# Two-layer image kernel: the odd groups' products with C go to buffers of their own, one pair of groups later

## Chip, core and metric

The kernel runs on one core of one Trainium2 chip. The metric is the device time of one execution in microseconds (us). Before the change three runs gave 21083.03, 21088.51 and 21097.53 us, so the median is 21088.51 us. All arithmetic is in 32-bit floats.

## The reference, cut to what matters

There are 16 images of 64x64 positions with 96 channels, and two layers, each added to its input after a group normalisation. Layer 0 resamples the image, passes it through a matrix, a quadratic and a second matrix, and resamples it back. Layer 1 is a selective scan in four directions; its core is all that the change touches:

```python
delta = softplus(dts + dt_bias)                    # per channel and position
def step(h, (dt, u, b, c)):                        # one position after another
    h = exp(dt * A) * h + (dt * u) * b             # 192 channels x 16 states, 4 directions
    y = sum_n(h * c)                               # read out with C
    return h, y
...
y = y0 + y2 reversed + (y1 + y3 reversed, turned)  # 4 directions of 4096 positions
out = layernorm(y) * silu(z) @ out_proj
```

So there are three large elementwise works per state and position: the drive (dt * u) * b, the recurrence over positions, and the product of h with c, which is then summed over the states.

## The kernel before, in words

**Tiles.** A tile of the scan has 128 partitions and T = 1024 positions: 32 channels times 4 of the 16 states. The work is cut into units (list `units`): one image has 8 steps (4 stretches of 1024 positions forwards, then 4 backwards), a step has 6 blocks, a block 4 units j = 0 to 3, one for each quarter of the states. A unit holds a pair of groups, e = 1 ("odd") and e = 0 ("even"), 32 channels each. That makes 192 units for an image and 3072 in all.

**What a unit n does.** The order of emission in the unit's loop is the order on every engine; nothing rearranges it.

- `decay` (L785): ScalarE writes exp(delta * A) for one group into a PSUM tile `da0` or `da1`; there is one of each.
- `drive` (L791): GpSimd writes (dt * u) * b for both groups into one tile `b` of 128x2048, two units ahead. Four such tiles rotate (`sc_4`).
- `recur` (L797): VectorE runs the recurrence, a scan instruction at L803 (forwards) or L805 (backwards), first for the odd group, in place into `b`, then for the even group, in place into `da0`.
- Product with C: the even group's is VectorE's (L972). The odd group's is GpSimd's (L963), in place in `b`, save in each fifth unit or so (`odd_here`; `SHARE` = 5), where it is VectorE's (L954); there the odd scan writes into `da1`.
- `keep` (L807): the last column of h is copied into `new`, the starting state of the next step. For the even group, and for the odd one when `odd_here`, ScalarE copies; otherwise VectorE does. The last step of a direction keeps nothing.
- `read_out(n - 1)` (L813): TensorE sums the products of the unit before over the states, with 16 matmuls (L827) into the PSUM tile `y`.

Other work is fed into these queues in small slices at three places of each unit (`slot`): the next image's layer 0, normalisations and convolution (`front`), the last stage of the image before (`finish`), and the projections of the next step (`project`). `slot` also picks extra units for `odd_here` around the convolution (`full_unit`). Loads and stores all go through SyncE's queue, in order: `fetch_dtu`, `fetch_delta`, `fetch_bc` (tiles `bt` and `ct`, five each). A load into a tile still in use waits in that queue, and all later loads and stores with it.

On GpSimd unit n is thus: product of n (L963), drive of n+2 (L794). On VectorE: odd scan, copy, even scan, even product, with the slices' small instructions between them; among these `norm` has one 96x1 product `nb` (L237), twice for an image.

Of the kernel before, what the change touches and what calls it, by code (L numbers as in the profile page):

```python
# [45 lines left out]
F32 = mybir.dt.float32  # L46
# [16 lines left out]
T = 1024  # L63
NT = L // T
NQ = 4
QT = T // NQ
# [14 lines left out]
def tile_two_blocks(  # L81
# [4 lines left out]
    nc = tc.nc  # L86
# [21 lines left out]
    fold_s = load(fold, "fold_s")  # L108
# [509 lines left out]
    blocks = [(0, 0, 0), (0, 2, 0), (2, 0, 0), (2, 2, 1), (1, 0, 1), (1, 2, 1)]  # L618
# [4 lines left out]
    def scan():  # L623


        with ExitStack() as es:
# [1 line left out]
            up_ = es.enter_context(tc.tile_pool(name="sc_u", bufs=4))  # L628
            cp = es.enter_context(tc.tile_pool(name="sc_bc", bufs=5))
            p3 = es.enter_context(tc.tile_pool(name="sc_3", bufs=3))  # L630
            p4 = es.enter_context(tc.tile_pool(name="sc_4", bufs=4))
            p2 = es.enter_context(tc.tile_pool(name="sc_2", bufs=2))
            yp = es.enter_context(tc.tile_pool(name="sc_y", bufs=1))
            stp = es.enter_context(tc.tile_pool(name="sc_st", bufs=2))
# [96 lines left out]
            def fetch_bc(ctx, r, j, what):  # L731
                t = cp.tile([128, T], F32, name="bt" if what == 0 else "ct")
                first = NS * what + NQ * j
                nc.sync.dma_start(
                    out=t, in_=ctx["rows"][r, first:first + NQ, :].unsqueeze(0).to_broadcast([32, NQ, T])
                )
                return t
# [8 lines left out]
            units = [(si_, bi, j) for si_ in range(len(steps)) for bi in range(len(blocks)) for j in range(NQ)]  # L746
            per_step = len(blocks) * NQ
            per_image = len(once) * per_step
            ctxs = [{} for _ in steps]

            bc, dtus, deltas = {}, {}, {}
# [28 lines left out]
                v, s0, r = blocks[bi]  # L780
                return 2 * steps[st][1] + r, s0 + e if v < 2 else 4 + e

            das, bs = {}, {}

            def decay(n, e):  # L785
                k, g = group(n, e)
                da = aps.tile([128, T], F32, name="da", tag=f"da{e}")
                nc.scalar.activation(da, deltas[n // NQ, e], AF.Exp, scale=a_s[:, k, g, units[n][2]:units[n][2] + 1])  # L788
                das[n, e] = da

            def drive(n):  # L791
                b = p4.tile([128, 2, T], F32, name="b")
                bt = bc[0, blocks[units[n][1]][2], units[n][2]]
                nc.gpsimd.tensor_mul(b, dtus[n // NQ], bt.unsqueeze(1).to_broadcast([128, 2, T]))  # L794
                bs[n] = b
# [8 lines left out]
                else:  # L804
                    nc.vector.tensor_tensor_scan(out[:, ::-1], da[:, ::-1], b[:, ::-1], before, ALU.mult, ALU.add)  # L805

            def keep(n, e, h, copy):  # L807
                st, bi, j = units[n]
                if st % NT < NT - 1:
                    end = h[:, T - 1:T] if steps[st][1] == 0 else h[:, 0:1]  # L810
                    copy(states[bi][1][:, e, j:j + 1], end)  # L811

            def read_out(n):  # L813
                st, bi, j = units[n]
                _, pair, lc = steps[st]
                if j == 0:
                    ys[n // NQ] = yps.tile([128, 2, QT], F32, name="y")
                y = ys[n // NQ]
                if j == 0 and pair == 1:
                    nc.tensor.matmul(  # L820
                        y.rearrange("p e t -> p (e t)"), lhsT=ident_s, rhs=y0s.pop((lc, bi)), start=True,
                        stop=False, skip_group_check=True,
                    )
                b = bs.pop(n)
                for e in range(2):
                    for q in range(NQ):
                        nc.tensor.matmul(  # L827
                            y[32 * q:32 * q + 32, e, :], lhsT=fold_s, rhs=b[:, e, QT * q:QT * q + QT],
                            start=(pair == 0 and j == 0 and e == 0), stop=(j == NQ - 1), skip_group_check=True,
                        )  # L830

# [50 lines left out]
            def slot(position):  # L882
                nonlocal full, full_unit
                back = ahead_gen if ahead_gen.gen is not None else behind_gen
                back.at += 1
                step_gen.at += 1
                gate = back.said == WAIT and back.due() and position == 2 and storing is None
                if gate:
                    full, full_unit = 2, n + 1
                if step_gen.due() and not (full and step_gen.said == BUSY):  # L890
                    light = step_gen.said != BUSY
                    step_gen.step()

                    if light and step_gen.due() and step_gen.said != BUSY:
                        step_gen.step()
                if back.due() and (gate or back.said != WAIT):
                    back.step()
                full = max(full - 1, 0)

            last = len(units) - 1  # L900
# [10 lines left out]
                drive(n)  # L911
            for e in range(2):
                decay(0, e)
            storing, credit = None, 0

            for n, (st, bi, j) in enumerate(units):
                mi, pair, lc = steps[st]
                v, s0, r = blocks[bi]
                m = n // NQ
                if n % per_image == 0:  # L920
                    image[mi]["y"] = dram.tile([2, DI, L], F32, name="y_d")
                    behind_gen.drain()
                    ahead_gen = behind_gen = nothing
                    if mi + 1 < B:
                        ahead_gen = Background(front(mi + 1), SLICES, POS)
                elif n % per_image == 2 and mi > 0:
                    behind_gen = Background(finish(mi - 1), SLICES, POS)
                if j == 0:
                    new = stp.tile([128, 2, NQ], F32, name="new", tag=f"st{bi}")
                    states[bi] = (states[bi][1] if states[bi] else None, new)  # L930

                if j == 0:
                    ahead = None
                    if bi + 1 < len(blocks):
                        ahead = ctxs[st], bi + 1
                    elif n + NQ <= last:
                        step_gen.drain()
                        ahead = ctxs[st + 1], 0
                        next_step(st + 2, mi)
                    if ahead:  # L940
                        dtus[m + 1] = fetch_dtu(*ahead)
                elif j == 1:
                    if ahead:
                        deltas[m + 1, 1] = fetch_delta(*ahead, 1)


                credit += 1
                odd_here = n == full_unit or credit >= SHARE
                if odd_here:
                    credit -= SHARE  # L950
                h = das[n, 1] if odd_here else bs[n][:, 1, :]
                recur(n, 1, h)
                if odd_here:
                    nc.vector.tensor_mul(bs[n][:, 1, :], h, bc[1, r, j])  # L954
                keep(n, 1, h, nc.scalar.copy if odd_here else nc.vector.tensor_copy)
                if n < last:
                    decay(n + 1, 1)
                slot(0)
                if storing is not None:
                    next(storing, 0)  # L960
                    storing = None
                if not odd_here:
                    nc.gpsimd.tensor_mul(h, h, bc[1, r, j])  # L963
                if n + 2 <= last:
                    drive(n + 2)

                h = das[n, 0]
                recur(n, 0, h)
                if n >= 1:
                    read_out(n - 1)  # L970
                slot(1)
                nc.vector.tensor_mul(bs[n][:, 0, :], h, bc[1, r, j])  # L972
                keep(n, 0, h, nc.scalar.copy)
                if n < last:
                    decay(n + 1, 0)
                if n >= 1 and units[n - 1][2] == NQ - 1:
                    storing = store(n - 1)
                    next(storing)
                slot(2)
                if j == 2 and ahead:  # L980
                    deltas[m + 1, 0] = fetch_delta(*ahead, 0)
                if j == NQ - 1 and n < last and steps[units[n + 1][0]][1] == 1:
                    st2, bi2, _ = units[n + 1]
                    y0s[steps[st2][2], bi2] = fetch_y0(steps[st2][2], bi2)


                at = n % per_step
                for what in range(2):
                    ahead_j = at - (2 * NQ - 1 + what)
                    if 0 <= ahead_j < NQ:  # L990
                        bc[what, 1, ahead_j] = fetch_bc(ctxs[st], 1, ahead_j, what)
                    ahead_j = at - (5 * NQ - 1 + what)
                    if 0 <= ahead_j < NQ and st + 1 < len(steps):
                        bc[what, 0, ahead_j] = fetch_bc(ctxs[st + 1], 0, ahead_j, what)
            read_out(last)
            for _ in store(last):
                pass
# [110 lines left out]
```

## Time and profile before

| | us |
|---|---|
| Median of three runs | 21088.51 |
| Profiled execution, span from the first to the last instruction | 21083.6 |
| First and last scan instruction start, in the span | 494.0 and 20914.9 |
| GpSimd busy, VectorE busy, TensorE busy, ScalarE busy | 19498.8, 19569.4, 16908.7, 13780.9 |
| Drives, 3072 of them, mean | 4.532 |
| GpSimd's products, 2458 of them, mean | 2.358 |
| VectorE's even products, 3072, mean | 1.223 |
| Columns copied by VectorE, 1844, mean | 0.154 |
| Mean granted TensorE clock | 0.860 of full |

A group's row gives its busy time and the mean of one instruction, and after the bar the idle time of the engine just before it, with what ended that idle time. Instructions of an engine overlap a little at their ends, so the time that one costs in a full queue is the distance between the starts of its neighbours, which the timeline shows, not its own length. 3072 units lie in some 20425 us, which makes 6.649 us for one.

### The profile page before, as it was taken

The page shows a single profiled execution, that of the slowest core. Times are in us where ns is not written, and L with a number is a line of the kernel's source. Part 1 is how long each engine was busy: PE and PEld are TensorE (multiplying, and loading weights), DVE is VectorE, ACT ScalarE, POOL GpSimd, SP SyncE. Part 2 cuts the span into 40 slices and gives each one's busy share as a digit, 9 for nine tenths or more (in the row PEclk, how much of TensorE's full clock was granted, in tenths as well). Part 3 has the DMA queues.
Part 4 walks back from the last instruction along what each step waited for, and adds up shares of the span by engine and source line. Part 5 has one row for each costly group of instructions (what it writes and reads, how often), then busy time and mean ns, then how long its engine had stood idle before and what let it go on. Part 6 is the DMA issues. An engine that isn't in the chain of part 4 may idle for free. (4 is left out here: it accounts for less than half of the span.)

```text
span 21083.6 us, 273452 instructions
## 1 busy us (share of the span) xinstructions
PE 16908.7 (80%) x98988; PEld 7230.6 (34%) x98988; DVE 19569.4 (93%) x12983; ACT 13780.9 (65%) x20546; POOL 19498.8 (92%) x5538
## 2 busy tenths in 40 slices
PE   7876788888878788788788888888787787888856
PEld 4423324233343333324333242333433333243221
DVE  0999999999999999999999999999999999999997
ACT  4666666667666666666666666676666666666553
POOL 0999999999999999999999999999999999999996
PEclk8887888888889888898888988888898888988977
DMA  2565565655656566565665656556565665656654
GB/s 84 191 202 195 195 227 195 221 202 196 226 198 227 197 210 212 194 230 191 218 207 197 226 199 219 202 197 222 197 226 198 212 212 198 229 195 216 224 186 141
DMA packets 1855464, 4277.11 MB, mean 203 GB/s; under 512 B 449438, under 2 KB 548670, under 8 KB 1852062
## 3 DMA queue, kind: packets, MB, share of 16 engines
q1 hardware_dynamic: 1854110, 4259.62, 60.1%
q8 instruction: 781, 12.80, 0.3%
q14 instruction: 573, 4.69, 0.1%
HBM read 3380.58 MB, written 878.18 MB: 202 GB/s over the span
## 5 line engine op out<-in xcount | busy, mean ns | idle before, releaser
L794 POOL TENSOR_TENSOR b<-dtu,bt 128x2048 f32<-128x2048 f32 x3072 | 13895.8, 4532 | 581.2 <-DMA dtu<-dtu_d 465.1
L788 ACT ACTIVATE da<-delta,a_s 128x1024 f32<-128x1024 f32 x6144 | 6857.4, 1117 | 2562.1 <-DVE b L972 945.5
L963 POOL TENSOR_TENSOR b<-b,ct 128x1024 f32<-128x1024 f32 x2458 | 5797.1, 2358 | 836.9 <-DVE new L811 628.6
L827 PE MATMUL y<-b,fold_s 128*32 128x256 f32 x49152 | 3871.3, 437 | 1153.0 <-DVE b L972 680.8
L972 DVE TENSOR_TENSOR b<-da,ct 128x1024 f32<-128x1024 f32 x3072 | 3756.4, 1223 | 91.8
L803 DVE TENSOR_TENSOR_SCAN da<-da,new,b 128x1024 f32<-128x1024 f32 x1383 | 3245.3, 2347 | 72.7 <-ACT da L788 57.2
L805 DVE TENSOR_TENSOR_SCAN da<-da,new,b 128x1024 f32<-128x1024 f32 x1361 | 3193.0, 2346 | 99.7 <-ACT da L788 77.0
L827 PEld LDWEIGHTS y<-b,fold_s 128*32 128x32 f32 x49152 | 1388.5, 119 | 3876.9 <-issue 1464.0
L805 DVE TENSOR_TENSOR_SCAN b<-da,new,b 128x1024 f32<-128x1024 f32 x943 | 2208.7, 2342 | 139.3 <-ACT da L788 81.5
L803 DVE TENSOR_TENSOR_SCAN b<-da,new,b 128x1024 f32<-128x1024 f32 x921 | 2156.5, 2341 | 11.2 <-ACT da L788 10.5
L811 ACT COPY new<-da 128x1 f32<-128x1 f32 x2764 | 432.9, 157 | 2607.4 <-DVE b L972 2236.0
L488 PE MATMUL c_ps<-xgp,wtap_s 96*64 96x512 f32 (+1 forms) x4608 | 1728.2, 633 | 184.7 <-ACT row L506 179.4
L697 PE MATMUL s<-w,ident_s 128*128 128x512 f32 x1530 | 1167.2, 854 | 636.0 <-ACT w L692 614.2
L371 PE MATMUL h_ps<-xu,w1t_s 96*128 96x500 f32 x1920 | 1044.0, 643 | 299.9 <-ACT t L311 125.9
L383 PE MATMUL o_ps<-w2c_s,hsq 128*100 128x96 f32 x9600 | 1041.5, 266 | 178.1 <-ACT hsq L352 177.8
L677 PE MATMUL s<-pr,dtw_s 128*128 128x512 f32 x1530 | 928.5, 691 | 315.2 <-ACT delta L703 224.9
L805 DVE TENSOR_TENSOR_SCAN da<-da,b 128x1024 f32<-128x1024 f32 x482 | 1103.5, 2289 | 53.0 <-ACT da L788 43.1
L383 PEld LDWEIGHTS o_ps<-w2c_s,hsq 128*100 128x100 f32 x9600 | 975.0, 179 | 410.3 <-ACT hsq L352 232.1
L803 DVE TENSOR_TENSOR_SCAN da<-da,b 128x1024 f32<-128x1024 f32 x460 | 1053.0, 2289 | 36.8 <-ACT da L788 34.8
L697 PE MATMUL s<-e,ident_s 128*128 128x512 f32 x1530 | 1004.2, 745 | 0.0
L820 PE MATMUL y<-y,ident_s 128*128 128x512 f32 x768 | 524.2, 770 | 583.5 <-ACT yt L838 457.6
L488 PEld LDWEIGHTS c_ps<-xgp,wtap_s 96*64 96x64 f32 (+1 forms) x4608 | 583.1, 169 | 1121.7 <-issue 842.6
(143 smaller groups left out, 21936.5 us busy)
## 6 DMA issues: line engine op xcount, KB each, us to landing
dtu<-dtu_d SPq DMA_DIRECT2D x1536, 512.0 KB
delta<-delta_d SPq DMA_DIRECT2D x1536, 512.0 KB
bt<-rows SPq DMA_DIRECT2D x1024, 512.0 KB
ct<-rows SPq DMA_DIRECT2D x1024, 512.0 KB
u<-xs_d SPq DMA_DIRECT2D x893, 256.0 KB
dtu_d<-dtu SPq DMA_DIRECT2D x765, 256.0 KB
delta_d<-delta SPq DMA_DIRECT2D x765, 256.0 KB
xr<-in_x SPq DMA_DIRECT2D x768, 128.0 KB
```

The lines of the kernel that those rows point to most:

```text
L371: nc.tensor.matmul(h_ps[j], lhsT=w1t_s[:, 128 * j:128 * (j + 1)], rhs=xu.rearrange("c p q -> c (p q)"), start=True, stop=True,)
L383: nc.tensor.matmul(o_ps[:, p, :], lhsT=hsq[j][:, UPS * p:UPS * (p + 1)], rhs=w2c_s[:, j, :], start=(j == 0), stop=(j == HB - 1),)
L488: nc.tensor.matmul(c_ps[p:p + n], lhsT=wtap_s[:, tap, 128 * i:128 * i + n], rhs=xgp[:, h0:h0 + 8, dx:dx + HW], start=(tap == 0), stop=(tap ...
L677: nc.tensor.matmul(s, lhsT=dtw_s[:, pair, v, :], rhs=pr, start=True, stop=True)
L697: nc.tensor.matmul(s, lhsT=ident_s, rhs=of, start=(k == 0), stop=(k == 3))
L788: nc.scalar.activation(da, deltas[n // NQ, e], AF.Exp, scale=a_s[:, k, g, units[n][2]:units[n][2] + 1])
L794: nc.gpsimd.tensor_mul(b, dtus[n // NQ], bt.unsqueeze(1).to_broadcast([128, 2, T]))
L803: nc.vector.tensor_tensor_scan(out, da, b, before, ALU.mult, ALU.add)
L805: nc.vector.tensor_tensor_scan(out[:, ::-1], da[:, ::-1], b[:, ::-1], before, ALU.mult, ALU.add)
L827: nc.tensor.matmul(y[32 * q:32 * q + 32, e, :], lhsT=fold_s, rhs=b[:, e, QT * q:QT * q + QT], start=(pair == 0 and j == 0 and e == 0), sto ...
L963: nc.gpsimd.tensor_mul(h, h, bc[1, r, j])
L972: nc.vector.tensor_mul(bs[n][:, 0, :], h, bc[1, r, j])
```

## The change

1. The odd group's product by GpSimd is no longer in place. `weigh` writes it into a tile `p` of its own (pool `sc_p`, two tiles of 128x1024). It is issued one unit later, and behind the drive: unit n on GpSimd is now drive of n+2, product of n-1.
2. The read-out follows one unit later: `read_out(n - 2)` takes the even half from `b` and the odd half from `p` (or from `b`, where VectorE made it). With it go the store of a block's result, the start of `finish`, and the loads of the second half's `ct` tiles, which come one unit later; the loads of the next step's `ct` tiles stay where they were.
3. `sc_4` has five drive tiles instead of four.
4. ScalarE copies all last columns. For an odd group that GpSimd multiplies, the copy comes behind the decay of unit n+1.
5. The space set aside for dynamically made DMA descriptors is 1024 bytes.

```diff
-            p4 = es.enter_context(tc.tile_pool(name="sc_4", bufs=4))
+            p4 = es.enter_context(tc.tile_pool(name="sc_4", bufs=5))
+            pp2 = es.enter_context(tc.tile_pool(name="sc_p", bufs=2))
...
-            def keep(n, e, h, copy):
+            def keep(n, e, h):
                 st, bi, j = units[n]
                 if st % NT < NT - 1:
                     end = h[:, T - 1:T] if steps[st][1] == 0 else h[:, 0:1]
-                    copy(states[bi][1][:, e, j:j + 1], end)
+                    nc.scalar.copy(states[bi][1][:, e, j:j + 1], end)
+
+            def weigh(n):
+
+                _, bi, j = units[n]
+                if n not in on_vector:
+                    prods[n] = pp2.tile([128, T], F32, name="p")
+                    nc.gpsimd.tensor_mul(prods[n], bs[n][:, 1, :], bc[1, blocks[bi][2], j])
...
                 b = bs.pop(n)
+                parts_of = b[:, 0, :], prods.pop(n, b[:, 1, :])
...
-                            y[32 * q:32 * q + 32, e, :], lhsT=fold_s, rhs=b[:, e, QT * q:QT * q + QT],
+                            y[32 * q:32 * q + 32, e, :], lhsT=fold_s, rhs=parts_of[e][:, QT * q:QT * q + QT],
...
-                elif n % per_image == 2 and mi > 0:
+                elif n % per_image == 3 and mi > 0:
...
                 if odd_here:
                     credit -= SHARE
+                    on_vector.add(n)
...
-                keep(n, 1, h, nc.scalar.copy if odd_here else nc.vector.tensor_copy)
+                    keep(n, 1, h)
                 if n < last:
                     decay(n + 1, 1)
+                if not odd_here:
+                    keep(n, 1, h)
...
-                if not odd_here:
-                    nc.gpsimd.tensor_mul(h, h, bc[1, r, j])
                 if n + 2 <= last:
                     drive(n + 2)
+                if n >= 1:
+                    weigh(n - 1)
...
-                if n >= 1:
-                    read_out(n - 1)
+                if n >= 2:
+                    read_out(n - 2)
                 slot(1)
                 nc.vector.tensor_mul(bs[n][:, 0, :], h, bc[1, r, j])
-                keep(n, 0, h, nc.scalar.copy)
+                keep(n, 0, h)
...
-                if n >= 1 and units[n - 1][2] == NQ - 1:
-                    storing = store(n - 1)
+                if n >= 2 and units[n - 2][2] == NQ - 1:
+                    storing = store(n - 2)
...
-                    ahead_j = at - (2 * NQ - 1 + what)
+                    ahead_j = at - (2 * NQ - 1 + 2 * what)
...
+            weigh(last)
+            read_out(last - 1)
             read_out(last)
...
-    nc = bacc.Bacc("TRN2", target_bir_lowering=False, num_devices=1)
+    nc = bacc.Bacc("TRN2", target_bir_lowering=False, num_devices=1, dynamic_dma_scratch_size=1024)
```

More of the change, by code (lines that the diff above doesn't have):

```diff
@@ L781, in group @@
                 return 2 * steps[st][1] + r, s0 + e if v < 2 else 4 + e
-            das, bs = {}, {}
+            das, bs, prods = {}, {}, {}
             def decay(n, e):
@@ L913, in scan @@
                 decay(0, e)
-            storing, credit = None, 0
+            storing, credit, on_vector = None, 0, set()
             for n, (st, bi, j) in enumerate(units):
```

## The prediction

> **What bounds the kernel now.** I read the busy times of the engines first, then the groups, the waits of VectorE and GpSimd, and the timeline for the distances between starts.
>
> ```profile
> span 21083.6 us, 273452 instructions
> PE 16908.7 (80%) x98988; PEld 7230.6 (34%) x98988; DVE 19569.4 (93%) x12983; ACT 13780.9 (65%) x20546; POOL 19498.8 (92%) x5538
> ```
>
> Two engines are over nine tenths busy, GpSimd (POOL) and VectorE (DVE). No single one is full, so the question is what each waits for.
>
> ```profile
> POOL b L963 <- DVE new L811: 628.6, 296, 14.1
> POOL b L794 <- DMA dtu<-dtu_d: 465.1, 1, 465.1
> ...
> DVE dtu L702 <- PE s L697: 335.8, 108, 141.3
> DVE da L805 <- ACT da L788: 120.1, 115, 4.2
> DVE b L805 <- ACT da L788: 98.7, 69, 3.7
> DVE da L803 <- ACT da L788: 92.0, 85, 2.1
> DVE b L805 <- POOL b L794: 51.9, 92, 0.9
> DVE da L805 <- POOL b L794: 30.2, 42, 0.9
> ```
>
> Columns: total us, times, longest. GpSimd waits for the odd scan and its copied column (628.6). VectorE waits for GpSimd's drives only 101 us in all (51.9, 30.2 and two rows of 14.2 and 4.9). It waits for ScalarE's decays 334 us (the three rows and one of 23.6) and for TensorE's s 194 (335.8 less the one wait of 141.3 before the scan part). So inside the scan part VectorE is more often the late one, and most of its own waits are for engines that the change hardly relieves.
>
> ```profile
> 8002.47 4.54 POOL L794 TENSOR_TENSOR b<-dtu,bt 128x2048 f32<-128x2048 f32 x1
> 8002.64 0.15 DVE L811 COPY new<-b 128x1 f32<-128x1 f32 x1
> 8002.71 2.35 DVE L805 TENSOR_TENSOR_SCAN da<-da,new,b 128x1024 f32<-128x1024 f32 x1
> ...
> 8082.72 2.34 DVE L805 TENSOR_TENSOR_SCAN b<-da,new,b 128x1024 f32<-128x1024 f32 x1
> 8084.98 2.33 DVE L805 TENSOR_TENSOR_SCAN da<-da,new,b 128x1024 f32<-128x1024 f32 x1
> ```
>
> Columns: start, length. The first three lines show a copy between two scans and under a running drive. The last two show the scans of a last step, with no copy: 2.26 us from start to start.
>
> **What each engine needs.** GpSimd's product and drive repeat each 6.82 us where it never rests, and a drive alone takes 4.49. 2458 x 6.82 + 614 x 4.49 = 19520 us, of the 20425 of the scan part. The change leaves every one of these instructions; a product out of place should cost like half a drive (4.532 / 2 = 2.27 against 2.36 in place), so between -0.09 and 0 each; I take 0.
>
> VectorE needs 20425 less its waits, some 680 in the scan part (101 + 334 + 194 and about 50 in the last stage's products), so 19745. It is the busier of the two by 225 us, and gets shorter by the copies.
>
> **The change part by part.**
>
> *Copies leave VectorE.* From the odd scan's start to the even scan's start it takes 2.356 (mean, scan to copy) + 0.071 (middle value, copy to scan) = 2.427 us with a copy (1844 cases), and 2.257 without one (middle value of 510). 1844 x 0.170 = 313 us. The built program puts a wait in front of the even scan, for the product of the pair before. In 135 scan pairs of the trace such a waiting instruction stands between, and they lie 2.257 apart too: nothing.
>
> Here a rule speaks for a far greater gain. The Trainium skill, page "SBUF — State Buffer", section on SBUF's two sides, says that VectorE and GpSimd share one port pair under an exclusive lock, that a 32-bit copy within SBUF on VectorE asks for it, and that the loser stands still for the whole instruction. By that a copy under a drive waits for half of it or so, 2 us, and 1844 of them would be worth over 3000 us. The row of all 1844 copies says 153/154/157 ns (least, middle, most), under running drives too. I take the row: 313.
>
> *How much of the 313 arrives.* I cut the 14 middle images by the starts of their odd scans. In units 110 to 143 of an image (the convolution) VectorE waits 16.8 us an image for ScalarE and TensorE; 23 of an image's 115 copies lie there, and I count half of those as lost to the same waits, 23 x 16 x 0.17 / 2 = 31. Leaves 282.
>
> *Copies arrive on ScalarE.* 1844 x 0.157 = 290 us, on an engine that is 65% busy, behind the decay of n+1, which waits for the same scan. Queued behind it are the slice's work, the even copy and the even decay, for which VectorE's next even scan waits. VectorE found a decay late 295 times in 3072 units, one in ten: 29 us. If ScalarE had no slack anywhere it would be 290, if it always had, 0.
>
> *The product one unit later, behind the drive, in `p`.* Before, GpSimd can't begin product n until odd scan n is done, and the drive of n+2 stands behind it. After, a product has a unit more on both sides, and so has the drive. The products' wait of 628.6 mostly goes, but that alone gives nothing where VectorE is the late one. What it gives is VectorE's 101 us on drives. They arise where GpSimd runs without a rest: in units 144 to 169 an image takes 177.3 us with 175.6 of GpSimd's work, while just before, in 110 to 143, GpSimd idles 30.4. One unit of lead carried over covers most of these waits; I take 60 (0 to 101).
>
> *The read-out one unit later.* TensorE's 49152 matmuls stay. Before, it waits 772 us (weight loads) for L972's products just made; these waits shrink. Behind them in its queue are the slices' matmuls, which feed ScalarE and so the decays. That may shorten VectorE's 334 + 194; I count 0, and up to half, 265, as a rival. *The fifth drive tile*: the drive of n+2 takes the tile of n-3, whose read-out now stands in the same unit n-1 as that of n-2 did, so its cover is the same; the row is 87.6 us of GpSimd waiting for y. *The scratch space*: all loads are issued by SyncE, no row of GpSimd makes any; nothing.
>
> *What the lead does to `nb`.*
>
> ```profile
> L237 DVE TENSOR_TENSOR nb<-nmean,rg x32: 156/5728/12324, 38.7 to 19074.5; 96x1 f32<-96x1 f32 x32
> ```
>
> A 96x1 product takes 5.7 us in the middle and 12.3 at most, against 0.156 in the first image, where GpSimd is idle. The same page's lock covers VectorE instructions with two SBUF inputs, as this one has. By the rule it waits for one GpSimd instruction, 4.5 us at most, and a greater lead changes nothing. The timeline says more: at 7560.16 it lasts 8.14, through the rest of one drive, a product and a whole drive, and ends when GpSimd has run out of work that it may do. Thus it grows with the lead that GpSimd still has to use up. If GpSimd is mostly ahead already, by nothing; if it is just in time, by a unit and more, some 9 us, 30 x 9 = 270. VectorE being the busier, I take 1 us each, 30.
>
> *SyncE.* The next step's `ct` loads stay put while the product that frees their tile comes a unit later; see the third rival. I count 0.
>
> **Sum.** 282 + 60 - 29 - 30 = 283 less. Against the profiled 21083.6: 20801; the median of the runs is 5 above it, so 20806.
>
> **The rivals.**
>
> *More is freed* (12%): TensorE no longer waits for fresh products, and half of VectorE's 529 us on decays and s goes too. 20806 - 265 = 20541. For it: the 772 us. Against: in the convolution those waits end at ScalarE's table loads and TensorE's long matmuls, not at read-outs.
>
> *Nothing arrives* (15%): the copies' time comes back as waits for decays (up to 290), or `nb` grows by its 270. 20806 + 270 = 21076. For it: ScalarE's 334 us already there. Against: it idles a third of the time.
>
> *SyncE stalls, slower* (13%). Place: the ends of units 21, 22 and 23 of each step, where a `ct` load waits for GpSimd's product of the unit before; that wait is there now, 128 times, 75.2 us in all. Behind it stands the load of the even `delta`, due about a unit later. If GpSimd runs just in time for VectorE, the product comes up to 13.6 us later against the drives than before (drive and product twice). Then the even decay is late and VectorE with it. At 4 us a step, 128 x 4 = 512, the time is 21318. It decides from 283 / 128 = 2.2 us a step. Against: GpSimd ahead, SyncE has no wait at all; ScalarE waits for delta now only 123.9 us.
>
> **How the numbers follow.** The sum's case has 57%, with its own range 20650 to 20980 (copies' half lost or not, 0 to 101, `nb` 0 to 4 us). The rivals have 12, 15 and 13, and 3 are left for what I don't see, slower. Ten in a hundred are cut above by leaving part of the slow case out, and the low end reaches into the first rival: 20590 to 21140. A measurement tells 0.2%, 42 us, from no change. Faster: 56 of the sum's, 12, and 3 of "nothing arrives", 71%. Same: 11. Slower: 13 + 3 + 2 = 18.
>
> **What would show it.** No VectorE copy at the keep line, and odd and even scans 2.26 apart. GpSimd's wait at the products under 200 us, VectorE's at drives under 60. A mean unit of 6.56. `nb` in the middle below 8 us. VectorE's waits for decays between 300 and 400. It is wrong if SyncE's wait for GpSimd at the `ct` loads runs to hundreds of us, if `nb` doubles, or if GpSimd's product without an in-place output takes longer than 2.36.

## The result, and the profile after

The changed kernel takes 21261.57 us (median of four runs, 21229.12 to 21282.86) against 21089.54 for the kernel before (four runs, 21083.03 to 21097.53): 172 us more, a ratio of 1.0079 with a 95% interval of 1.0065 to 1.0094. The forecast was 20806, so the sign was wrong and the time lies above the range. The profiled execution spans 21251.1 us.

The page of the kernel after, its span and busy times:

```profile
span 21251.1 us, 276431 instructions
...
PE 16859.1 (79%) x98988; PEld 7219.9 (34%) x98988; DVE 19357.3 (91%) x11139; ACT 13934.5 (66%) x22390; POOL 19499.3 (92%) x5538
```

VectorE (DVE) has 1844 instructions less than before and is busy for 212 us less (19569.4 before): the copies' 283.8 us are gone, but its `nb` products take 101 more. GpSimd's work is the same. Both now stand still for longer: over the scan part VectorE idles 1160 us instead of 717 (gaps of over 0.05 us, summed from the trace), GpSimd 1098 instead of 929 (all its gaps). The change took work off the busier engine and put more idle time in its place.

The waits of the kernel after (total us, times, longest), a few rows of each engine:

```profile
DVE da L806 <- ACT da L789: 380.6, 262, 11.1
DVE dtu L703 <- PE s L698: 364.9, 134, 140.3
...
DVE da L804 <- ACT da L789: 179.3, 184, 4.2
...
DVE b L806 <- ACT da L789: 103.6, 89, 3.1
...
DVE yz L588 <- ACT sq L584: 83.2, 38, 4.1
...
DVE sq L603 <- issue: 63.7, 14, 5.1
...
DVE b L804 <- ACT da L789: 12.7, 11, 3.3
...
DVE b L806 <- POOL b L795: 8.0, 13, 0.9
...
POOL b L795 <- PE y L836: 540.6, 181, 9.7
...
POOL p L819 <- DVE b L804: 7.2, 3, 2.4
...
ACT da L789 <- DMA delta<-delta_d: 296.2, 113, 11.1
...
PE y L836 <- POOL p L819: 1434.5, 639, 9.3
...
SPq L857 <- ACT yt L847: 1926.0, 307, 21.9
SPq L735 <- POOL p L819: 1392.2, 325, 14.5
```

L804 and L806 are the scans, L789 the decay, L795 the drive, L819 the product into `p`, L836 the read-out, L735 the loads of `bt` and `ct`, L857 the store of a block's result in the backward steps, L588 and L603 a product and a sum of the last stage. Rows of the kernel before that the prediction doesn't show:

```profile
POOL b L794 <- PE y L827: 87.6, 30, 3.8
...
ACT da L788 <- DMA delta<-delta_d: 123.9, 56, 5.3
...
PE y L827 <- DVE b L972: 680.8, 277, 12.8
...
PE y L827 <- POOL b L963: 167.1, 136, 5.3
...
SPq L848 <- ACT yt L838: 1310.3, 295, 18.8
...
SPq L734 <- POOL b L963: 75.2, 128, 3.0
```

Side by side:

- What the change was to remove is gone. GpSimd's wait at its products went from 628.6 to 7.2, VectorE's wait for drives from 101 to 11.
- VectorE now waits 676 us for ScalarE's decays (the four rows with `da L789`), where it waited 334.
- TensorE waits 1434.5 us for GpSimd's products, where it waited 167.1 for them and 680.8 for VectorE's even products, which hold up only its weight loads now (208 us, 772 before). GpSimd's drives now wait 540.6 us for TensorE's read-outs, where it was 87.6.
- VectorE's waits at L588 and L603, in the last stage, came to 206 us (the two rows and two of 31.8 and 27.2), where they were 76.
- ScalarE waits 296.2 us for the loads of `delta`, where it was 123.9; in SyncE's queue the `ct` loads wait 1392.2 for GpSimd's products (75.2 before), and the stores 1926.0 for their result (1310.3).

Where this falls in an image can be had from the starts of the odd scans. Means of the 14 middle images, us:

| Units of an image | before | after | what runs there |
|---|---|---|---|
| 0 to 47 | 317.6 | 317.1 | start, layer 0 of the next image |
| 48 to 95 | 306.8 | 306.9 | layer 0 |
| 96 to 109 | 98.8 | 104.1 | second `norm`, with `nb` at unit 101 |
| 110 to 143 | 235.8 | 231.1 | convolution |
| 144 to 169 | 177.3 | 188.3 | GpSimd without a rest |
| 170 to 191 | 143.2 | 144.6 | end of the image |
| all | 1279.4 | 1292.2 | |

The convolution gained 4.7 us an image. Units 144 to 169 lost 11.0, 96 to 109 lost 5.3. The single unit that lost most is 144, the border between two steps: 9.3 us before, 15.8 after. Unit 101, with `nb`, is among the next: 14.6 before, 19.3 after. The timeline of the kernel before at that border (start, length, and in brackets the idle time before it and its cause):

```profile
7844.91 2.16 SPq L848 DMA_DIRECT2D y_d<-yt  x4
...
7854.74 0.52 SPq L715 DMA_DIRECT2D delta<-delta_d  x1
...
7857.98 2.34 DVE L805 TENSOR_TENSOR_SCAN b<-da,new,b 128x1024 f32<-128x1024 f32 x1
...
7862.73 2.15 ACT L788 ACTIVATE da<-delta,a_s 128x1024 f32<-128x1024 f32 x2 [4.46 <-DMA delta<-delta_d]
7863.88 2.36 DVE L805 TENSOR_TENSOR_SCAN da<-da,new,b 128x1024 f32<-128x1024 f32 x1 [3.36 <-ACT da L788]
```

And of the kernel after, at the same place of the same image:

```profile
7906.06 2.34 DVE L806 TENSOR_TENSOR_SCAN b<-da,new,b 128x1024 f32<-128x1024 f32 x1
7906.26 4.07 SPq L857 DMA_DIRECT2D y_d<-yt  x4
...
7908.32 2.33 DVE L806 TENSOR_TENSOR_SCAN da<-da,new,b 128x1024 f32<-128x1024 f32 x1
...
7911.83 2.34 DVE L806 TENSOR_TENSOR_SCAN b<-da,new,b 128x1024 f32<-128x1024 f32 x1
...
7915.46 0.53 SPq L716 DMA_DIRECT2D delta<-delta_d  x1
...
7921.69 2.15 ACT L789 ACTIVATE da<-delta,a_s 128x1024 f32<-128x1024 f32 x2 [9.26 <-DMA delta<-delta_d]
7922.85 2.36 DVE L806 TENSOR_TENSOR_SCAN da<-da,new,b 128x1024 f32<-128x1024 f32 x1 [8.68 <-ACT da L789]
```

The first and third lines show the promised 2.26 us from odd to even scan. Then see the order in SyncE's queue. Before, the store of the last block went out 9.8 us ahead of the even `delta` load, and that load 3.2 us ahead of the odd scan at the border. After, the store goes out a unit later, the load comes 9.2 us behind it again, which is now 3.6 us after the odd scan, and the even scan stands still for 8.7 us.

### The profile page after: what moved, and what is told of

It is laid out like the page before. It is cut to its first block, busy times and chain, and to the rows that moved or that the text cites. A ratio compares the mean times of both kernels' runs of the same rounds, so it can differ in the third digit from the quotient of the medians.

```text
span 21251.1 us, 276431 instructions
## 1 busy us (share of the span) xinstructions
PE 16859.1 (79%) x98988; PEld 7219.9 (34%) x98988; DVE 19357.3 (91%) x11139; ACT 13934.5 (66%) x22390; POOL 19499.3 (92%) x5538
## 5 line engine op out<-in xcount | busy, mean ns | idle before, releaser
L795 POOL TENSOR_TENSOR b<-dtu,bt 128x2048 f32<-128x2048 f32 x3072 | 13933.3, 4543 | 1580.3 <-DMA dtu<-dtu_d 582.0
L789 ACT ACTIVATE da<-delta,a_s 128x1024 f32<-128x1024 f32 x6144 | 6845.7, 1116 | 2612.4 <-DVE b L984 914.1
L819 POOL TENSOR_TENSOR p<-b,ct 128x1024 f32<-128x1024 f32 x2458 | 5822.8, 2369 | 7.2 <-DVE b L804 7.2
L806 DVE TENSOR_TENSOR_SCAN da<-da,new,b 128x1024 f32<-128x1024 f32 x1361 | 3187.4, 2342 | 309.6 <-ACT da L789 309.6
L804 DVE TENSOR_TENSOR_SCAN da<-da,new,b 128x1024 f32<-128x1024 f32 x1383 | 3239.1, 2342 | 127.6 <-ACT da L789 120.0
L836 PE MATMUL y<-p,fold_s 128*32 128x256 f32 x19664 | 1768.1, 436 | 1435.6 <-POOL p L819 1434.5
L836 PE MATMUL y<-b,fold_s 128*32 128x256 f32 x29488 | 2466.4, 427 | 155.6 <-ACT yt L847 155.3
L806 DVE TENSOR_TENSOR_SCAN b<-da,new,b 128x1024 f32<-128x1024 f32 x943 | 2207.3, 2341 | 106.8 <-ACT da L789 97.5
L804 DVE TENSOR_TENSOR_SCAN b<-da,new,b 128x1024 f32<-128x1024 f32 x921 | 2156.7, 2342 | 18.2 <-ACT new L812 9.5
L488 PE MATMUL c_ps<-xgp,wtap_s 96*64 96x512 f32 (+1 forms) x4608 | 1659.5, 611 | 64.8 <-ACT row L506 59.5
L836 PEld LDWEIGHTS y<-b,fold_s 128*32 128x32 f32 x29488 | 716.0, 115 | 2086.3 <-issue 1094.5
L836 PEld LDWEIGHTS y<-p,fold_s 128*32 128x32 f32 x19664 | 607.0, 119 | 2202.8 <-POOL p L819 1849.2
L667 PE MATMUL pp<-u,xpt_s 128*128 128x512 f32 x1530 | 968.0, 781 | 372.6 <-DMA u<-xs_d 269.4
L806 DVE TENSOR_TENSOR_SCAN da<-da,b 128x1024 f32<-128x1024 f32 x482 | 1100.9, 2284 | 72.0 <-ACT da L789 71.0
L804 DVE TENSOR_TENSOR_SCAN da<-da,b 128x1024 f32<-128x1024 f32 x460 | 1049.9, 2282 | 66.4 <-ACT da L789 59.3
```

What stands on the lines that cost most here:

```text
L488: nc.tensor.matmul(c_ps[p:p + n], lhsT=wtap_s[:, tap, 128 * i:128 * i + n], rhs=xgp[:, h0:h0 + 8, dx:dx + HW], start=(tap == 0), stop=(tap ...
L667: nc.tensor.matmul(pp, lhsT=xpt_s[:, pair, v, :], rhs=u[v], start=(v == 0), stop=(v == 2))
L804: nc.vector.tensor_tensor_scan(out, da, b, before, ALU.mult, ALU.add)
L819: nc.gpsimd.tensor_mul(prods[n], bs[n][:, 1, :], bc[1, blocks[bi][2], j])
L836: nc.tensor.matmul(y[32 * q:32 * q + 32, e, :], lhsT=fold_s, rhs=parts_of[e][:, QT * q:QT * q + QT], start=(pair == 0 and j == 0 and e == ...
```

## The experiments

The change is two things: a relief (own tile, fifth drive tile, copies on ScalarE) and a delay by one unit (product, read-out, store and loads). Three suspects stood against each other: the delay, through SyncE's queue or TensorE's; `nb`, by waiting for GpSimd; and the copies, by burdening ScalarE. In the expectations, S stands for SyncE's queue at the `ct` loads, D for the store ahead of the `delta` load, P for TensorE standing at the late product, N for `nb`. Differences to the kernel after are differences of medians; with half intervals of 0.001 to 0.0015 on each side they are uncertain by some 35 to 45 us (0.0015 of 21090 is 32, and two of them make 45). The median of the kernel before was 21090.35 in the runs with `ct_later`, `nb_scalar`, `cols_alone` and `own_now`, 21092.48 in those with `prod_first`, `delta_first`, `before_nb` and `own_nb`, and 21093.51 in those with the last four. Intervals are 95%.

**The next step's `ct` loads one unit later** (`ct_later`), as the change did for the second half's:

```diff
-                    ahead_j = at - (5 * NQ - 1 + what)
+                    ahead_j = at - (5 * NQ - 1 + 2 * what)
                     if 0 <= ahead_j < NQ and st + 1 < len(steps):
                         bc[what, 0, ahead_j] = fetch_bc(ctxs[st + 1], 0, ahead_j, what)
+                if at == 0 and st > 0:
+                    bc[1, 0, NQ - 1] = fetch_bc(ctxs[st], 0, NQ - 1, 1)
```

> The changed kernel, with the next step's ct loads one unit later too, as the second half's are. Theory S (SyncE's queue stands at these loads, waiting for the late product, and the delta loads behind it come late): SyncE's wait for the product there falls from 1392 us to under 300, VectorE's idle time at the step border (unit 144 of an image, 9.9 us) falls to about 3, and the time is 21100 to 21160. Theories N (the nb product is locked out longer by GpSimd's lead) and P (TensorE stands at the late product and holds back the slices' matmuls): time within 0.2% of the changed kernel, 21220 to 21300.

Measured: 21202.61, ratio 1.0057 (1.0042 to 1.0072), 59 us less than the kernel after. SyncE's waits at the `ct` loads, in its own list of waits:

```profile
SPq L735 <- POOL p L819: 480.2, 233, 5.6
```

The wait fell by 912 us and the time by 59; neither expected range holds it. The `ct` loads are part of the cause, but a queue's wait is no measure of time: what stood behind most of this one can't have been urgent. Unit 144 still took 14.9 us (15.8), so what held the `delta` load there was not them.

**`nb` on ScalarE in the changed kernel** (`nb_scalar`):

```diff
-        nc.vector.tensor_mul(nb, nmean, rg)
+        nc.scalar.activation(nb, nmean, AF.Identity, scale=rg)
```

> The changed kernel, with the 96x1 product nb made by ScalarE instead of VectorE. Theory N: nb's 295 us leave VectorE and the stage around unit 101 is over 8 us shorter in each image; 21000 to 21130. Theories S and P: most of the time won turns into other waits; 21200 to 21260.

Measured: 21081.79, ratio 0.9996 (0.9987 to 1.0005), 180 us less than the kernel after. By itself this would make `nb` the whole loss. But VectorE's waits for decays are as long as in the kernel after (693 us), so it cured something else. What the kernel before gains by the same edit decides; see `before_nb`.

**The copies alone, in the kernel before** (`cols_alone`). ScalarE copies the odd column too, behind the next decay, except where VectorE makes the product:

```diff
-                    copy(states[bi][1][:, e, j:j + 1], end)
+                    nc.scalar.copy(states[bi][1][:, e, j:j + 1], end)
...
-                keep(n, 1, h, nc.scalar.copy if odd_here else nc.vector.tensor_copy)
+                    keep(n, 1, h)
                 if n < last:
                     decay(n + 1, 1)
+                if not odd_here:
+                    keep(n, 1, h)
```

> The kernel before, with ScalarE copying all last columns, as in the change, and nothing else; GpSimd's product in place now has to wait for that copy, which stands behind the decay. If the copies' 313 us are a real gain of VectorE: 20850 to 21000. If they come back as waits for ScalarE, or GpSimd's product waits for the copy: 21050 to 21250.

Measured: 21027.88, ratio 0.9972 (0.9963 to 0.9982), so 62 us faster than before, between the two expected ranges. Its waits:

```profile
POOL b L965 <- ACT new L811: 753.0, 437, 14.4
...
DVE b L805 <- POOL b L794: 174.5, 321, 1.1
...
DVE da L803 <- POOL b L794: 109.6, 163, 1.1
...
DVE da L805 <- POOL b L794: 55.9, 69, 1.1
```

The copies don't make the kernel as a whole slower: that rival falls. But of the 282 us counted for them 62 arrive. The in-place product must now wait until ScalarE has read the column (753 us, where the copy of VectorE had cost 628.6), GpSimd becomes the later one (a drive is done 1.0 us ahead of its odd scan in the middle, 2.4 before), and VectorE's waits for drives rise from 101 to 383 us (the three rows and one of 43), those for decays from 334 to 400. Even the 62 us are not the copies' own. The 30 later cases of `nb` fall from 194.7 to 85.5 us, and units 96 to 109 take 93.3 us an image instead of 98.8; the rest of an image takes 3.5 us longer than before (of which 1.3 stand for the profiled execution, 20 us above the median). So the gain lies at `nb`, and elsewhere the copies brought nothing.

**The relief without the delay** (`own_now`): product of n by GpSimd ahead of the drive again, read-out, store, loads and the start of `finish` as before; own tile, five drive tiles and the copies stay.

```diff
+                weigh(n)
                 if n + 2 <= last:
                     drive(n + 2)
-                if n >= 1:
-                    weigh(n - 1)
...
-                if n >= 2:
-                    read_out(n - 2)
+                if n >= 1:
+                    read_out(n - 1)
...
-                if n >= 2 and units[n - 2][2] == NQ - 1:
-                    storing = store(n - 2)
+                if n >= 1 and units[n - 1][2] == NQ - 1:
+                    storing = store(n - 1)
...
-                    ahead_j = at - (2 * NQ - 1 + 2 * what)
+                    ahead_j = at - (2 * NQ - 1 + what)
```

> The changed kernel without the delay: the product goes to its own tile p, but in the same unit ahead of the drive, the read-out is one unit later as before the change, ct loads as before; fifth drive tile and ScalarE's copies stay. If the lateness of the product is the cause (S, P or N): 20850 to 21050, faster than before. If ScalarE's copies are the cause: 21200 to 21300, with the waits for decays of the changed kernel.

Measured: 20978.01, ratio 0.9949 (0.9934 to 0.9964): 112 us faster than before, 284 faster than the kernel after. Its waits:

```profile
POOL p L819 <- DVE b L806: 485.2, 182, 13.0
...
POOL p L819 <- DVE b L804: 147.2, 75, 14.6
...
PE y L836 <- POOL p L819: 205.4, 165, 3.2
```

GpSimd waits 632 us at its products again (485.2 + 147.2), as much as in the kernel before, and the kernel is the faster one. So the delay is the harm, all of 284 us, and whatever the wait that it removed was worth, the delay cost more. Of the 282 us counted for the copies, 112 arrive: VectorE's waits for drives are 217 us here, where they were 101, and those for decays 427, where they were 334. What in the delay does the harm? The next runs take it apart.

**The product ahead of the drive, but still of the unit before** (`prod_first`):

```diff
-                if n + 2 <= last:
-                    drive(n + 2)
                 if n >= 1:
                     weigh(n - 1)
+                if n + 2 <= last:
+                    drive(n + 2)
```

> The changed kernel with GpSimd's two instructions of a unit in the other order: product of n-1 first, then the drive of n+2. Everything else stays a unit later. Theory P (TensorE stands at the late product, and with it the slices' matmuls and the decays): TensorE's wait for p falls from 1434 us to under 500, VectorE's waits for decays from 676 to about 450, time 21060 to 21160. If the order on GpSimd doesn't matter (N and D alone): 21220 to 21300.

Measured: 21172.31, ratio 1.0039 (1.0024 to 1.0054), 89 us less than the kernel after and just above the expected range. TensorE's wait for products, and VectorE's in the last stage:

```profile
PE y L836 <- POOL p L819: 322.2, 152, 6.2
...
DVE yz L588 <- ACT sq L584: 41.7, 24, 3.9
```

TensorE's fell from 1434.5 us, and SyncE's at the `ct` loads from 1392.2 to 619.4. ScalarE's wait for `delta` did not change (298.5 for 296.2). Units 144 to 169 take 183.1 us an image (188.3), with the idle time at single units there gone: unit 154 from 3.0 us to 0.2, unit 166 from 4.5 to 1.0. This is a second cause, apart from the loads: behind a 4.5 us drive the product comes late for the read-out, TensorE stands in front of it, and the slices' matmuls, emitted behind it, are late. What VectorE no longer waits for are mostly these slices: at L588 and L603 its waits fall from 206 to 83 us. Its waits for decays fall from 676 to 627 only, not to the expected 450, and those for drives rise from 11 to 153. So that the order on GpSimd costs 89 us is shown; that it does so through late slices follows from where the waits went, and the path over the decays is the smaller part of it.

**The even `delta` load ahead of the store** (`delta_first`): in the block's unit j = 2 the load is issued behind the odd decay, in front of the store, no longer at the unit's end.

```diff
+                if j == 2 and ahead:
+                    deltas[m + 1, 0] = fetch_delta(*ahead, 0)
                 slot(0)
                 if storing is not None:
                     next(storing, 0)
...
                 slot(2)
-                if j == 2 and ahead:
-                    deltas[m + 1, 0] = fetch_delta(*ahead, 0)
```

> The changed kernel with the even delta load of the next block issued right after the odd decay in unit j = 2, ahead of the store of the block before, instead of at the unit's end. Theory D (the store, one unit later since the change, now stands in SyncE's queue ahead of this load and holds it up): ScalarE's waits for delta fall from 296 us to under 130, VectorE's idle time at unit 144 of an image from 9.9 to 3 or 4 us, time 21100 to 21190. Otherwise 21230 to 21290, with unit 144 as it was.

Measured: 21149.17, ratio 1.0030 (1.0018 to 1.0041), 112 us less than the kernel after. ScalarE's wait for the load:

```profile
ACT da L789 <- DMA delta<-delta_d: 76.1, 58, 3.0
```

By the medians this is the largest of the three causes. The wait for `delta` falls from 296.2 us. SyncE's wait at the stores (L857) falls from 1926.0 to 29.8: it now waits at the `delta` load until the tile is free, and the store behind it finds its result made. Unit 144 takes 8.7 us. A part of the stall moves on: in unit 147 VectorE idles 7.0 us where it idled 0.2, waiting for a decay. Over units 110 to 143 an image gains 4.7 us (231.1 to 226.4).

**`nb` on ScalarE in the kernel before** (`before_nb`), with the diff of `nb_scalar`:

> The kernel before, with nb made by ScalarE. It gives nb's price without the change. If nb's whole price of 180 us in the changed kernel comes from GpSimd's greater lead: 21070 to 21100. If nb costs the kernel before what its 195 us say, and the change only adds to that: 20920 to 21000, and what the change adds is the difference to 180.

Measured: 20930.50, ratio 0.9926 (0.9910 to 0.9943), 162 us less than before. So of the 180 us that the edit brought in the changed kernel, 162 lay in the kernel before as well. The change made `nb` dearer by some 18 us, which these intervals can't tell from nothing.

**Relief without delay, and `nb` on ScalarE** (`own_nb`), the two diffs together:

> The version without the delay (own tile for the product, fifth drive tile, ScalarE's copies; 20978 us) with nb made by ScalarE. If nb's lock and the delay are separate causes the two gains add up: 20800 to 20900. If nb's gain turns into waits for decays: 20930 to 20980.

Measured: 20816.63, ratio 0.9870 (0.9855 to 0.9885). It is 161 us faster than `own_now`: the two gains add.

**The three cures of the delay together** (`three`): `ct_later`, `prod_first` and `delta_first`, `nb` as it was.

> The changed kernel with three of the single edits together: next step's ct loads one unit later, GpSimd's product ahead of the drive, even delta load ahead of the store. If S, P and D are separate parts of the delay's price, 59 + 90 + 113 = 262 go: 21000, as the version without the delay (20978). If they are the same stalls seen three times, 21080 to 21150.

Measured: 21032.69, ratio 0.9971 (0.9960 to 0.9982), 229 us less than the kernel after, between the two expected times. The single gains (59, 89 and 112) make 260, so they are mostly separate. It stays 55 us behind `own_now`. One wait is there that neither `own_now` nor any of the three single cures has:

```profile
DVE b L986 <- DMA ct<-rows: 76.8, 27, 5.1
```

Here L986 is the even product: at the start of a step a moved `ct` load now comes too late for VectorE. Its size would fit the 55 us, but so would `nb`: unit 101 takes 19.6 us an image, 14.7 in `own_now`. The next run decides between them.

**The same with `nb` on ScalarE** (`four`):

> The same three edits and nb made by ScalarE. Without GpSimd's lead into nb: the time of the three-edit version less 160 to 190 (nb's price before the change was 162, in the changed kernel 180).

Measured: 20784.64, ratio 0.9851 (0.9836 to 0.9866), the fastest of all. The wait for `ct` is still there:

```profile
DVE b L986 <- DMA ct<-rows: 76.6, 27, 5.1
```

Yet this kernel is not slower than `own_nb` (20816.63), the version without the delay and with the same `nb`: 32 us less, within the intervals of both. So the 55 us by which `three` stays behind `own_now` lay at `nb` and not in the wait for `ct`: of the 5.2 us that an image of its profiled execution is longer, unit 101 has 5.0.

The edit on `nb` gives 248 us here (21032.69 less 20784.64), more than expected, where `own_now` gained 161 by it. The difference of 87 us is uncertain by some 60 (the four half intervals, squared, added and the root taken). The 30 later cases of `nb` take 304.3 us in `three` and 197.5 in `own_now`. Units 96 to 109 take 90.7 us with the edit, 104.4 without. In the kernel after, `nb` is held for nearly as long as in `three` (295.4 us) and the edit gives only 180; why the rest doesn't show there was not tested.

Seen from the other side: with `nb` on ScalarE the three edits bring 297 us (`nb_scalar` 21081.79 less 20784.64), and leaving out the delay brings 265 (21081.79 less 20816.63). So late `ct` loads, late product, late store and `nb` are the whole price of the delay, within the noise.

**The best version without delay, with the `delta` load ahead of the store** (`own_nb_delta`), the diffs of `own_nb` and `delta_first`:

> The version without the delay, nb made by ScalarE (20817), and the even delta load ahead of the store. ScalarE still waits 183 us for delta there; if those waits count: 20740 to 20800, else 20800 to 20830.

Measured: 20806.34, ratio 0.9865 (0.9848 to 0.9881). Against `own_nb` (20816.63) it is 10 us less, within the intervals of both. Where the store is not late, moving the load in front of it gives nothing that these runs can tell. So the 112 us of `delta_first` are the price of the late store, not a gain that lay open anyway.

**The buffers alone, in the kernel before** (`buf_alone`): five drive tiles and the smaller descriptor space.

```diff
-            p4 = es.enter_context(tc.tile_pool(name="sc_4", bufs=4))
+            p4 = es.enter_context(tc.tile_pool(name="sc_4", bufs=5))
...
-    nc = bacc.Bacc("TRN2", target_bir_lowering=False, num_devices=1)
+    nc = bacc.Bacc("TRN2", target_bir_lowering=False, num_devices=1, dynamic_dma_scratch_size=1024)
```

> The kernel before with five drive tiles instead of four and the space for dynamic DMA descriptors cut to 1024 bytes, nothing else. Costed at nothing: 21050 to 21130, within 0.2% of before; GpSimd's 88 us of waiting for y may go without moving the time.

Measured: 21082.19, ratio 0.9995 (0.9987 to 1.0004): no difference. GpSimd's 88 us of waiting for `y` are gone, and its wait at the products rises from 628.6 to 706.5 us.

## Why the prediction was wrong

The forecast was 283 us less, and it came to 172 more: 455 us to explain. They split in two by `own_now`: the relief gave 112 instead of 253 (282 less 29), so 141 are missing there; the delay cost 284 instead of giving 30 (60 less 30), which is 314. 141 + 314 = 455.

| Term of the sum | forecast | shown by the runs |
|---|---|---|
| Copies off VectorE, onto ScalarE | -282 + 29 | -62 alone, and that at `nb`; -112 with own tile and fifth drive tile |
| GpSimd's lead | -60 | VectorE's waits for drives 101 to 11 us; lost in the cost of the delay |
| Product out of place | 0 | 2.369 us a product, 2.358 before |
| Read-out one unit later | 0, perhaps -265 | with the product behind the drive +89 |
| SyncE: `ct` loads | 0 | +59 |
| SyncE: the store ahead of the even `delta` load | not named | +112 |
| `nb` grows | +30 | +18 in the kernel after, +87 with the three stalls cured |
| Fifth tile, descriptor space | 0 | within noise, in the kernel before |

*What held.* The distance of the scans, the vanishing wait of GpSimd at its products, VectorE's waits for drives, the product's price, and the buffers. GpSimd did get its lead: a drive is done 5.9 us ahead of its odd scan in the middle, 2.4 before. None of this decides the time. Of the signs that it would be wrong the first one came: SyncE's wait for GpSimd at the `ct` loads ran to 1392 us. The middle `nb` is 9.0 us, where it was to stay below 8.

*First failed step: "I count 0" for SyncE.* The third rival named the right queue and the right victim, the even `delta` load, but the smaller of two culprits. The front part says that the store moves one unit with the read-out; I costed that for the `ct` loads alone and did not ask what stands behind a later **store**. It waits for ScalarE's copy of the result, and the even `delta` load, due within a unit, is behind it. `delta_first` gets 112 us back, `ct_later` 59. The rival's price was wrong too: I set 4 us a step for the `ct` loads and it was 59 / 128 = 0.46. That its 21318 lies near the measured time is luck. No one cause reached the 2.2 us a step from which I let it decide; the whole delay did (284 / 128 = 2.2).

*Second failed step: "these waits shrink" for TensorE.* I took it that a product with a unit more of time is done earlier against its read-out. But the read-out moved by the same unit, and the product moved behind a drive besides. It comes later against its read-out than before. The wait that I named did shrink (weight loads for the even product from 772 to 208 us), but TensorE's wait for GpSimd's product went from 167 to 1434 us. The slices' matmuls are emitted behind the read-out and are late with it, and VectorE waits for them in the last stage (76 us before, 206 after). Its waits for decays, which I hoped would get shorter, went from 334 to 676, of which the late product explains the smaller part (627 are left in `prod_first`). I had the sign of the effect wrong, and the reason for it stood in my own text ("behind the drive"). `prod_first` shows 89 us of it.

*Third failed step: "how much of the 313 arrives".* I looked for VectorE's waits for ScalarE and TensorE and took off 31 us. What took most of the gain was GpSimd. VectorE was only 225 us longer than GpSimd by my own account, and a gain of 282 on it must run into the other engine unless the wait between the two goes as well. `cols_alone` shows this (waits for drives 101 to 383); `own_now`, where the product no longer waits for the copy, gets 112, with 116 us more of waits for drives than before and 93 more for decays. Together these make more than the 141 us that are missing there. The 29 us set for ScalarE's part were too few as well: in `cols_alone`, where nothing but the copies moved, the waits for decays grew by 66. The lead that was to keep GpSimd from being late came only with the delay, and cost more than it brought.

*A term whose way was right and whose size stays open.* `nb` did grow with GpSimd's lead: its 30 later cases went from 194.7 to 295.4 us. Of these 101 us the time shows 18 in the kernel after, which is no more than noise, and 87 where the other three stalls are cured. So that 30 lies near 18 proves nothing. (The second rival's 21076 counts these 30 us twice; nothing hangs on it.) And I asked only how much it would grow. That it already cost 162 us in the kernel before could be had from the row that I quoted: 32 times about 6 us on an engine with hardly any idle time.

*What adds up, and what stays open.* The delay's 284 us: 112 + 89 + 59 and 18 for `nb` (180 less 161) make 278, with the uncertainty of each. This is a sum of single cures. Together the three give 229, and the 55 that are left went with `nb`, as `four` shows. What the copies cost on ScalarE was not separated from the rest (VectorE's waits on ScalarE's copies went from 8 to 80 us in the kernel after). How the 50 us between `cols_alone` and `own_now` divide among own tile and fifth drive tile was not tried.

## What to carry to other kernels

When a step is delayed, list every instruction that moves with it, its store above all, and for each in-order queue ask what stands behind it and when that is due; the wait that the delay removes must be one that the slowest chain really has, and removing 628 us of it brought no gain here. Where two engines are both over nine tenths busy, ask what relieves them together: here work taken off one alone turned mostly into waits for others. And look for tiny instructions with long times: moving 32 products of 96x1 to another engine gave 161 to 248 us, more than any other single edit in this study.

## What the runs showed of the hardware

**A small VectorE product can be held through several GpSimd instructions in a row.** The longest `nb` of the kernel after, in the timeline:

```profile
15358.61 2.33 POOL L819 TENSOR_TENSOR p<-b,ct 128x1024 f32<-128x1024 f32 x1
15359.31 15.16 DVE L237 TENSOR_TENSOR nb<-nmean,rg 96x1 f32<-96x1 f32 x1
15360.91 4.50 POOL L795 TENSOR_TENSOR b<-dtu,bt 128x2048 f32<-128x2048 f32 x1
...
15365.37 2.33 POOL L819 TENSOR_TENSOR p<-b,ct 128x1024 f32<-128x1024 f32 x1
15367.67 4.48 POOL L795 TENSOR_TENSOR b<-dtu,bt 128x2048 f32<-128x2048 f32 x1
15372.12 2.33 POOL L819 TENSOR_TENSOR p<-b,ct 128x1024 f32<-128x1024 f32 x1
15374.40 2.28 DVE L806 TENSOR_TENSOR_SCAN da<-da,b 128x1024 f32<-128x1024 f32 x1
```

The product begins under one GpSimd instruction and lasts through the whole of four more. GpSimd's instructions follow each other without a gap (each starts a little before the last ends), and only when the last of them ends at 15374.45, with no further one running, does the product end, at 15374.47. Its summary (least, middle and most of its duration in ns):

```profile
L237 DVE TENSOR_TENSOR nb<-nmean,rg x32: 155/9001/15164, 39.4 to 19238.0; 96x1 f32<-96x1 f32 x32
```

The Trainium skill, page "SBUF — State Buffer", section on SBUF's two sides, has the loser of the lock blocked while the other's instruction runs. The runs show more: up to five in a row. In the kernels before and after, in `own_now` and in `three`, all 30 later cases end 0.01 to 0.02 us after a GpSimd instruction, with none running behind it. It is no rule without exception: in `cols_alone` 18 of 30 end with one GpSimd instruction although the next has begun.

```profile
2436.10 4.53 POOL L794 TENSOR_TENSOR b<-dtu,bt 128x2048 f32<-128x2048 f32 x1
2437.59 3.05 DVE L237 TENSOR_TENSOR nb<-nmean,rg 96x1 f32<-96x1 f32 x1 [0.42 <-ACT rg L234]
...
2440.58 2.35 POOL L965 TENSOR_TENSOR b<-b,ct 128x1024 f32<-128x1024 f32 x1
```

Here the drive ends at 2440.63 and the product at 2440.64, where GpSimd's next product already runs. What decides between the two is open. On ScalarE the same product takes 0.28 us.

**A product out of place costs GpSimd no less than in place**: 2.369 us for 1024 positions against 2.358.

**ScalarE's copy of one column costs more from SBUF than from PSUM**: 0.176 us (mean of 1844, out of `b`) against 0.156 (mean of 2764, out of `da`). VectorE's copies had taken 0.154.
